# Key and query products of a graph-transformer layer from raw, feature-major rows, with the mean taken into the weights

## The chip, the cores and the metric

The kernel runs on one core of a Trainium2 chip. The metric is the device time of one execution in microseconds (us). A time is the median of several runs; a profile is one further execution, taken by the hardware profiler. The engines are TensorE (PE, with its weight loads as PEld), VectorE (DVE), ScalarE (ACT), GpSimd (POOL) and SyncE (SP), which only issues transfers. ACT and POOL issue transfers too.

## What is computed

One layer on N = 10000 nodes with D = 512 features, everything in 32-bit floats:

```python
xn  = layernorm(x)                       # no gamma; eps 1e-5
gnn = relu(segment_sum((xn @ W)[src] * edge_weight, dst) + bias)   # 160000 edges
q, k, v = split(xn @ w_qkv.T)            # 8 heads of 64
q = softmax(q over the 64 of its head) * 64**-0.5
k = softmax(k over the 10000 nodes)
mix = gamma_layernorm(((k.T @ v) per head applied to q) @ w_out.T)
x = x + gnn + mix
x = x + ffn(layernorm(x))                # two of eleven mixtures of six experts, gelu
```

## The kernel before

The nodes are cut into 20 chunks of 512 (the last has 272), each held as 128 partitions of 4 rows (`SUB`). The work runs in four stages.

**Early stage (chunks 0 and 1, `EARLY = 2`).** `normal_rows` loads a chunk of x, takes mean and variance of each row on DVE (`row_stats`), finishes the rate (variance + eps)^-0.5 and the shift on POOL, applies both on ACT (L422), and writes the normalised rows to `xn_d` in memory. It does so for all 20 chunks, seven buffers (`a_io`) turning over. Between these, DVE prepares the edge lists (`place_edges`), and the keys and queries of chunks 0 and 1 are made by plain products (`times`, L209).

**Key stage (chunks 2 to 19, line 856 on).** For each chunk the normalised rows are reloaded (`rows_of`), transposed on PE (`turned_rows`, which calls `transposed`, L201, and copies the result from PSUM to `xnT` on ACT and DVE, L203), and summed blockwise into `xs_b`. `seven` forms keys and queries with seven products instead of eight, from `xnT`, `xs_b`, the weights `wk` and `wq` and their blockwise sums `kq_sum`. ACT exponentiates, DVE adds keys up (`kacc`) and normalises queries. The next chunk's rows are then transposed, and the context `G` takes `ek` transposed times `xn` (`pc`, L911). Midway the queries are transposed and put away in `qT_d`.

The factor `usable` that scales the exponentials is 1 where the squared column norms of `wk` and `wq` are small enough for exponentials without a maximum, and 0 otherwise, when a general path recomputes everything.

**Attention stage.** The context is folded with the value and output weights; then for each chunk: queries times that (`po`), the collected messages times the graph weights (`pg`), norms and sums.

**Feed-forward stage**, from about 2143 us to the end; the change does not touch it.

**The edges.** Messages are gathered in 1250 tiles of 128 edges by POOL (`edges_in`, L583, one indirect transfer each, from `xn_d`, 24 buffers), multiplied on PE by a selection matrix (`edges_summed`, L601, four tiles side by side) and written out as partial sums. They are spread over the key and attention stages by a count kept while the program is written: `work(us)` adds the nominal time of the products just issued to `done[1]`, and `edges_to` issues edge tiles until their number matches `done[1] / pace`:

```python
edges_to(groups_of(int(done[1] / pace[0])))
```

with 0.83 us for a product of [128x128] by [128x512], `PACE = 0.9` us a tile in the key stage and `ROW_PACE` in the attention stage. At the start of the key stage `done[1]` is set to minus 16 tiles. In the attention stage `far_enough(c)` also forces out the tiles that the gather of chunk c's sums needs. PE's instructions run in the order in which the program writes them; the order on the other engines and queues is a planner's.

Of the kernel before, what the change touches and what calls it, by code (L numbers as in the profile page):

```python
# [9 lines left out]
F32 = mybir.dt.float32  # L10
I32 = mybir.dt.int32
AF = mybir.ActivationFunctionType
ALU = mybir.AluOpType
# [4 lines left out]
P = 128  # L18
SQ = 32
SPARE = 10  # L20
SUB = 4
# [7 lines left out]
EARLY = 2  # L29
# [3 lines left out]
KEPT = 2  # L33
PRODUCT = 0.83
PACE = 0.9
ROW_PACE = 0.96
LATE = 4
MIXED = 3

# [17 lines left out]
def gps_layer_kernel(  # L57
    ctx: ExitStack,
    tc: tile.TileContext,
    x: bass.AP,  # L60
    src: bass.AP,
    dst: bass.AP,
    edge_w: bass.AP,
# [13 lines left out]
    nc = tc.nc  # L77
# [21 lines left out]
    def tokens(t, c):  # L99
        b, r = chunks[c]  # L100
        return t[b : b + r * SUB, :].rearrange("(p s) d -> p s d", s=SUB)

    const = ctx.enter_context(tc.tile_pool(name="const", bufs=1))
    small = ctx.enter_context(tc.tile_pool(name="small", bufs=4))
    dram = ctx.enter_context(tc.tile_pool(name="dram", bufs=1, space=DRAM))
# [29 lines left out]
    row_of = const.tile([P, NCH], I32, name="row_of")  # L135
    msum = const.tile([P, 1], F32, name="msum")
    stats2 = const.tile([P, NCH, SUB, 2], F32, name="stats2")


    xn_d = dram.tile([N, D], F32, name="xn_d")  # L140
# [247 lines left out]
    with ExitStack() as ph:  # L388
# [15 lines left out]
        tmp = norm_ctx.enter_context(tc.tile_pool(name="edge_t", bufs=1))  # L404


        normal = []
        placing = []
        last_stats = [None]

        def normal_rows(n):

            for c in range(len(normal), min(len(normal) + n, NCH)):
                r = chunks[c][1]
                xt = (xp if c < KEPT else a_io).tile([P, SUB, D], F32, name="xn")
                nc.sync.dma_start(xt[:r], tokens(x, c))
                mv = small.tile([P, SUB, 2], F32, name="mv")
                last_stats[0] = row_stats(xt, r, mv, on_pool=True)
                nc.gpsimd.tensor_tensor(mv[:r, :, 0], mv[:r, :, 0], mv[:r, :, 1], ALU.mult)
                nc.gpsimd.tensor_scalar(mv[:r, :, 0], mv[:r, :, 0], -1.0, None, op0=ALU.mult)  # L420
                for i in range(SUB):
                    nc.scalar.activation(xt[:r, i, :], xt[:r, i, :], AF.Identity,  # L422
                                         bias=mv[:r, i, 0:1], scale=mv[:r, i, 1:2])
                nc.scalar.dma_start(tokens(xn_d, c), xt[:r])
                normal.append(xt)
                if len(normal) == LISTS:
                    placing.append(place_edges(*edges_listed()))
                for _ in range(2 if placing else 0):
                    next(placing[0], None)

        zero = tmp.tile([P, D], F32, name="zero")
        nc.vector.memset(zero, 0.0)
        nc.scalar.dma_start(part_d[ZERO_ROW : ZERO_ROW + P, :], zero)
        normal_rows(2)
        src_sb = ep.tile([P, NET], I32, name="src_sb")
        w_sb = ep.tile([P, NET], F32, name="w_sb")
# [172 lines left out]
        nexts = ep.tile([P, 1], F32, name="nexts")  # L609
        held = {"edges": []}  # L610

        def squares_of(w, tag):
            sq = b_io.tile([P, KB, D], F32, name="sq", tag=tag)
            nc.scalar.activation(sq, w, AF.Square)
            return sq

        def norms(i, sq):

            pn = psum_e.tile([P, KB], F32, name="pn", tag="pm")
# [78 lines left out]
        def work(us):  # L698
# [4 lines left out]
                normal_rows(int(done[1] / EARLY_TOTAL * (NCH + 1)) + 4 - len(normal))  # L703
                return
            edges_to(groups_of(int(done[1] / pace[0])))

        in_order = ph.enter_context(ExitStack())
        in_order.enter_context(tc.manual_schedule(engines={mybir.EngineType.PE}))

        def general_path():  # L710

# [122 lines left out]
            nc.sync.dma_start(xn[: chunks[c][1]], tokens(xn_d, c))  # L834
            return xn

        def turned_rows(c, xn):
            xnT = b_io.tile([P, KB, SUB * P], F32, name="xnT")
            transposed(xnT, xn, chunks[c][1], psum, "ps", by_act=range(KB) if c < EARLY else (1, 3))
            return xnT  # L840

        def finish(o, ek, r, at):
            if o is ek:
                nc.vector.tensor_tensor(kacc[:r], kacc[:r], ek[:r, at, :], ALU.add)
            else:
                softmax_rows(o, r, at)

        wk = kvp.tile([P, KB, D], F32, name="wk")
        nc.sync.dma_start(wk, w_qkv_t[:, D : 2 * D].rearrange("(k p) d -> p k d", p=P))
        nc.sync.dma_start(wq, w_qkv_t[:, :D].rearrange("(k p) d -> p k d", p=P))  # L850
        squared = [squares_of(wk, "qT"), squares_of(wq, "xs_b")]
        kq_sum = kvp.tile([P, 4, KH, D], F32, name="kq_sum", tag="wv_wo")
        normal_rows(2)
        xn = rows_of(0)
        xnT = turned_rows(0, xn)
        for c, (_, r) in enumerate(chunks):
            if c == EARLY:
                for _ in placing[0]:
                    pass
                norm_ctx.close()  # L860
                pools["w"] = edge_ctx.enter_context(tc.tile_pool(name="edge_w", bufs=3))
                done[1] = -16 * PACE
                pools["m"] = edge_ctx.enter_context(tc.tile_pool(name="edge_m", bufs=24,
                                                                 reuse_waits="tile"))
            if c + 1 < EARLY:
                xn_next = rows_of(c + 1)
            elif EARLY <= c < NCH - 1:
                xn_next = rows_of(c + 1)
            ek = b_io.tile([P, SUB, D], F32, name="ek")
            qt = b_io.tile([P, SUB, D], F32, name="qt")  # L870
            if c < EARLY:
                for o, w in ((ek, wk), (qt, wq)):
                    sums = []
                    for s in range(SUB):
                        po = psum.tile([P, D], F32, name="pk", tag="ps")
                        times(po, xnT, s, r, w)
                        work(KB * PRODUCT)
                        sums.append(po)
                        if c == s == 0 and o is ek:
                            norms(0, squared[0])  # L880
                            norms(1, squared[1])
                            as_they_are()
                        for i, po in enumerate(sums):
                            at = s + 1 - len(sums) + i
                            nc.scalar.activation(o[:r, at, :], po[:r], AF.Exp, scale=usable[:r])
                            finish(o, ek, r, at)
                        sums = []
            else:
                xs = b_io.tile([P, 4, KH, HALF], F32, name="xs_b")
                h = 2 * r  # L890
                sums_of([xs[:, i, :, :h] for i in range(4)], xnT[:, :KH, :h], xnT[:, KH:, :h],
                        xnT[:, :KH, h : 2 * h], xnT[:, KH:, h : 2 * h])
                for s in range(SUB // 2):
                    first = seven(ek, qt, s, r, xnT, xs, (wk, wq), kq_sum, lambda n: work(n * KH * PRODUCT))
                    s2 = s + SUB // 2
                    nc.scalar.activation(ek[:r, s, :], first, AF.Exp, scale=usable[:r])
                    nc.scalar.activation(ek[:r, s2, :], ek[:r, s2, :], AF.Exp, scale=usable[:r])
                    finish(ek, ek, r, s)
                    finish(ek, ek, r, s2)
                    for q in (s, s2):  # L900
                        nc.scalar.activation(qt[:r, q, :], qt[:r, q, :], AF.Exp, scale=usable[:r])
                        finish(qt, ek, r, q)
            if c + 1 == EARLY:
                normal_rows(NCH)
                xn_next = rows_of(c + 1)
            if c + 1 < NCH:
                xnT = turned_rows(c + 1, xn_next)
            for cb in range(KB):
                pc = psum.tile([P, D], F32, name="pc", tag="ps")
                for s in range(SUB):  # L910
                    nc.tensor.matmul(pc, ek[:r, s, cb * P : (cb + 1) * P], xn[:r, s, :],  # L911
                                     start=s == 0, stop=s == SUB - 1)
                if c:
                    added = nc.vector.tensor_tensor(G[:, cb, :], G[:, cb, :], pc, ALU.add)
                    if cb == 0:
                        first_added = added
                else:
                    nc.vector.tensor_copy(G[:, cb, :], pc)
                work(SUB * PRODUCT)
                if cb == KB // 2 - 1:  # L920
                    qT = b_io.tile([P, KB, SUB * P], F32, name="qT")
                    transposed(qT, qt, r, psum, "ps", by_act=range(KB) if c < EARLY else (1, 3))
                    nc.scalar.dma_start(qT_d[c], qT[:, :, : SUB * r])
            if c == CHECKED:
                next_nodes()
                oddities()
            if c >= CHECKED:
                find_rows(c, added)
                if c < 2 * CHECKED:
                    find_rows(c - CHECKED, added)  # L930
            if c == EARLY - 1:
                for inst in sums_for([kq_sum[:, i] for i in range(4)], wk[:, :KH], wq[:, :KH], wk[:, KH:], wq[:, KH:]):
                    behind(inst, first_added)
            if c + 1 < NCH:
                xn = xn_next
# [537 lines left out]
```

## Time and profile before

| | us |
|---|---|
| median of 3 runs | 3301.59 (3297.64 to 3308.94) |
| the profiled execution | 3518.48 |
| its span, first to last instruction | 3516.7 |
| PE / DVE / ACT / POOL busy in it | 3256.7 / 1766.5 / 831.1 / 1311.2 |
| mean granted PE clock | 0.961 of full |

The profiled execution is 217 us longer than the median of the runs; its durations serve for a sum over its own stages. A page's rows give, for each group of instructions, source line, engine, operation, tiles written and read, count, busy time and mean duration, then the idle time of the engine just before them and what ended it. Rows in order of time begin with start and duration in us. A busy PE is not PE at its peak, since matmuls are pipelined and their ends modelled, so distances from start to start are used here.

### The profile page before, as it was taken

What the parts mean: (1) busy time and instruction counts of PE and PEld (TensorE: products, weight loads), DVE (VectorE), ACT (ScalarE), POOL (GpSimd) and SP (SyncE); (2) the same over time, 40 slices, a digit from 0 to 9 for tenths busy, and PEclk for the clock granted to TensorE, in tenths of its full rate; (3) what the DMA queues carried; (4) which work ended last, traced back from release to release, by engine and by line L of the source; (5) the groups of instructions that cost most, each with busy time, mean ns of one, the idle gap of its engine ahead of it and who ended that gap; (6) DMA issues with size and microseconds to landing.
All of it is one profiled execution on the core that took longest, in us unless ns stands there. A gap on an engine that the chain in (4) does not pass through costs nothing. (4 is left out here: it accounts for less than half of the span.)

```text
span 3516.7 us, 36142 instructions
## 1 busy us (share of the span) xinstructions
PE 3256.7 (93%) x12819; PEld 1916.0 (54%) x12819; DVE 1766.5 (50%) x3902; ACT 831.1 (24%) x1674; POOL 1311.2 (37%) x1421
## 2 busy tenths in 40 slices
PE   6899998988999989898998988999999999999998
PEld 3433333333333333333333335888888888888886
DVE  6644445444444425564565557445445544544542
ACT  5321212121112112121222113222222222222221
POOL 3466666665666656676676630000000000000000
PEclk8999999999999979899999988999999999999999
DMA  9677777776777878898998882221212212122111
GB/s 392 235 217 249 227 247 248 254 223 208 227 223 243 247 275 318 313 332 293 318 336 301 294 268 61 60 75 58 60 57 76 60 49 84 49 60 73 60 37 38
DMA packets 216735, 654.39 MB, mean 186 GB/s; under 512 B 34425, under 2 KB 74361, under 8 KB 188831
## 3 DMA queue, kind: packets, MB, share of 16 engines
q0 software_dynamic: 104096, 354.29, 32.0%
q1 hardware_dynamic: 69992, 175.33, 15.2%
q10 hardware_dynamic: 42452, 122.31, 9.0%
q8 instruction: 105, 1.72, 0.2%
q14 instruction: 90, 0.74, 0.1%
HBM read 491.21 MB, written 166.63 MB: 187 GB/s over the span
## 5 line engine op out<-in xcount | busy, mean ns | idle before, releaser
L583 POOL DMA_INDIRECT msg<-xn_d,src_sb x1250 | 1229.9, 984 | 634.4 <-issue 287.2
L601 PE MATMUL pm<-msg,sel 128*32 128x512 f32 x2504 | 351.7, 617 | 54.5 <-issue 44.5
L911 PE MATMUL pc<-xn,ek 128*128 128x512 f32 (+1 forms) x640 | 306.5, 624 | 20.5 <-issue 15.0
L209 PE MATMUL po<-G,qT 128*128 128x512 f32 (+1 forms) x640 | 302.0, 613 | 13.0 <-issue 12.2
L209 PE MATMUL pg<-wq,aT 128*128 128x512 f32 (+1 forms) x640 | 301.3, 617 | 10.2 <-issue 9.0
L604 ACT COPY part<-pm 128x512 f32<-128x512 f32 x217 | 127.1, 586 | 733.9 <-PE pm L601 276.0
L601 PEld LDWEIGHTS pm<-msg,sel 128*32 128x32 f32 x2504 | 66.1, 110 | 302.7 <-issue 266.2
L209 PEld LDWEIGHTS pg<-wq,aT 128*128 128x128 f32 (+1 forms) x640 | 117.7, 192 | 195.7 <-issue 184.7
L911 PEld LDWEIGHTS pc<-xn,ek 128*128 128x128 f32 (+1 forms) x640 | 122.7, 199 | 177.4 <-issue 164.7
L209 PEld LDWEIGHTS po<-G,qT 128*128 128x128 f32 (+1 forms) x640 | 117.4, 191 | 185.6 <-issue 181.4
L243 PE MATMUL px<-xnT,w_sb 128*128 128x256 f32 (+1 forms) x800 | 204.6, 379 | 6.8 <-DVE u L1290 6.8
L243 PE MATMUL p<-kq_sum,xs_b 128*128 128x512 f32 (+1 forms) x432 | 201.4, 600 | 3.2 <-issue 2.4
L166 DVE BATCH_NORM_STATS2 st<-ot 128x6 f32<-128x512 f32 (+1 forms) x160 | 110.3, 689 | 178.5 <-issue 119.2
L243 PE MATMUL px<-w_sb,hh 128*128 128x256 f32 (+1 forms) x800 | 185.7, 379 | 0.0
L243 PE MATMUL py<-xs,w_sum 128*128 128x256 f32 (+1 forms) x800 | 185.3, 374 | 0.0
L243 PE MATMUL p<-wk,xnT 128*128 128x512 f32 (+1 forms) x288 | 148.1, 637 | 34.9 <-issue 26.7
L243 PE MATMUL py<-w_sum,hh 128*128 128x256 f32 (+1 forms) x800 | 179.2, 379 | 0.0
L589 DVE TENSOR_TENSOR sel<-iota_w,place 128x128 f32<-128x128 f32 (+2 forms) x217 | 74.5, 344 | 206.1 <-remote 86.2
L243 PEld LDWEIGHTS px<-xnT,w_sb 128*128 128x128 f32 x800 | 150.7, 192 | 29.9 <-DVE u L1290 10.0
L243 PEld LDWEIGHTS py<-w_sum,hh 128*128 128x128 f32 (+1 forms) x800 | 150.0, 188 | 22.7
L243 PEld LDWEIGHTS px<-w_sb,hh 128*128 128x128 f32 (+1 forms) x800 | 150.0, 188 | 22.7
L243 PEld LDWEIGHTS py<-xs,w_sum 128*128 128x128 f32 x800 | 149.8, 190 | 19.9
(298 smaller groups left out, 4577.4 us busy)
## 6 DMA issues: line engine op xcount, KB each, us to landing
part_d<-part ACTq DMA_DIRECT2D x217, 256.0 KB
msg<-xn_d,src_sb POOLq DMA_INDIRECT x1250
xn<-in_x SPq DMA_DIRECT2D x19, 1024.0 KB
xn_d<-xn ACTq DMA_DIRECT2D x19, 1024.0 KB
qT_d<-qT ACTq DMA_DIRECT2D x19, 1024.0 KB
qT<-qT_d SPq DMA_DIRECT2D x19, 1024.0 KB
xt<-in_x SPq DMA_DIRECT2D x19, 1024.0 KB
x_d<-ot SPq DMA_DIRECT2D x19, 1024.0 KB
```

The source lines that it names most:

```text
L166: nc.vector.bn_stats(st[:r, s, :], t[:r, s, :])
L209: nc.tensor.matmul(po[:r, :], t[:, kb, s * r : (s + 1) * r], w[:, kb, :], start=kb == 0, stop=kb == KB - 1)
L243: nc.tensor.matmul(o, lhs[j], rhs[j], start=start and j == 0, stop=stop and j == n - 1, skip_group_check=True)
L583: nc.gpsimd.indirect_dma_start(out=m[k], out_offset=None, in_=xn_d, in_offset=bass.IndirectOffsetOnAxis(ap=src_sb[:, t0 + k : t0 + k + 1], ...
L589: nc.vector.tensor_tensor(sel[:, :n], iota_w[:, None, :].to_broadcast([P, n, WIN]), place[:, t0 : t0 + n, None].to_broadcast([P, n, WIN]), ...
L601: nc.tensor.matmul(pm[h * WIN : (h + 1) * WIN, :], sel[:, k, :], m[k] if k < len(m) else m[0], start=j == 0, stop=j == batch - 1, skip_gro ...
L604: nc.scalar.copy(part, pm)
L911: nc.tensor.matmul(pc, ek[:r, s, cb * P : (cb + 1) * P], xn[:r, s, :], start=s == 0, stop=s == SUB - 1)
```

## The change

The host now also hands over `x_t`, the values of x laid out by feature: for each chunk and each block of 128 features one row per feature, the tokens in the chunk's own order. `turned_rows` no longer transposes; it loads 1 MB of `x_t` into `xnT`. These rows are raw. Since k = rate * (x - mean(x)) @ W, the mean is moved to the weights: `centred` subtracts from each column of `wk` and `wq` its mean over the 512 features (a product with `all_ones`, then four updates on DVE). The rate of each token, kept in `stats1`, becomes the scale of the exponentials, multiplied by `usable`. The weights and the first chunk of `x_t` are loaded ahead of the normalised rows. The normalised rows themselves are still made, for the edges and for `pc`. Two constants of the edge schedule change: minus 49 tiles at the start of the key stage instead of minus 16, and `ROW_PACE` 0.94 instead of 0.96.

```diff
-ROW_PACE = 0.96
+ROW_PACE = 0.94
...
+    def columns(t, c):
+        b, r = chunks[c]
+        return t[:, KB * b : KB * (b + r * SUB)].rearrange("p (k n) -> p k n", k=KB)
...
+    stats1 = const.tile([P, NCH, SUB, 2], F32, name="stats1")
+    nc.gpsimd.memset(stats1, 0.0)
...
-                mv = small.tile([P, SUB, 2], F32, name="mv")
+                mv = stats1[:, c]
                 last_stats[0] = row_stats(xt, r, mv, on_pool=True)
...
+        def turned_rows(c):
+            xnT = b_io.tile([P, KB, SUB * P], F32, name="xnT")
+            nc.sync.dma_start(xnT[:, :, : SUB * chunks[c][1]], columns(x_t, c))
+            return xnT
+
+        def centred(w):
+
+            pcol = psum.tile([P, D], F32, name="pcol", tag="ps")
+            for kb in range(KB):
+                nc.tensor.matmul(pcol, all_ones, w[:, kb, :], start=kb == 0, stop=kb == KB - 1)
+            for kb in range(KB):
+                nc.vector.scalar_tensor_tensor(w[:, kb, :], pcol, -1.0 / D, w[:, kb, :], op0=ALU.mult, op1=ALU.add)
+
         zero = tmp.tile([P, D], F32, name="zero")
         nc.vector.memset(zero, 0.0)
         nc.scalar.dma_start(part_d[ZERO_ROW : ZERO_ROW + P, :], zero)
+        wk = kvp.tile([P, KB, D], F32, name="wk")
+        nc.sync.dma_start(wk, w_qkv_t[:, D : 2 * D].rearrange("(k p) d -> p k d", p=P))
+        xnT = turned_rows(0)
+        nc.sync.dma_start(wq, w_qkv_t[:, :D].rearrange("(k p) d -> p k d", p=P))
+        squared = [squares_of(wk, "qT"), squares_of(wq, "xs_b")]
+        centred(wk)
         normal_rows(2)
...
-        def turned_rows(c, xn):
-            xnT = b_io.tile([P, KB, SUB * P], F32, name="xnT")
-            transposed(xnT, xn, chunks[c][1], psum, "ps", by_act=range(KB) if c < EARLY else (1, 3))
-            return xnT
...
-        wk = kvp.tile([P, KB, D], F32, name="wk")
-        nc.sync.dma_start(wk, w_qkv_t[:, D : 2 * D].rearrange("(k p) d -> p k d", p=P))
-        nc.sync.dma_start(wq, w_qkv_t[:, :D].rearrange("(k p) d -> p k d", p=P))
-        squared = [squares_of(wk, "qT"), squares_of(wq, "xs_b")]
         kq_sum = kvp.tile([P, 4, KH, D], F32, name="kq_sum", tag="wv_wo")
         normal_rows(2)
         xn = rows_of(0)
-        xnT = turned_rows(0, xn)
         for c, (_, r) in enumerate(chunks):
             if c == EARLY:
...
+                rates = ep.tile([P, NCH, SUB], F32, name="rates")
+                nc.vector.tensor_scalar(rates, stats1[:, :, :, 1], usable, None, op0=ALU.mult)
                 norm_ctx.close()
                 pools["w"] = edge_ctx.enter_context(tc.tile_pool(name="edge_w", bufs=3))
-                done[1] = -16 * PACE
+                done[1] = -49 * PACE
...
+                    if c == 0 and o is qt:
+                        centred(wq)
...
+                        if s == 0 and o is ek:
+                            rate = small.tile([P, SUB], F32, name="rate")
+                            nc.vector.tensor_scalar(rate[:r], stats1[:r, c, :, 1], usable[:r], None, op0=ALU.mult)
...
-                            nc.scalar.activation(o[:r, at, :], po[:r], AF.Exp, scale=usable[:r])
+                            nc.scalar.activation(o[:r, at, :], po[:r], AF.Exp, scale=rate[:r, at : at + 1])
...
-                    nc.scalar.activation(ek[:r, s, :], first, AF.Exp, scale=usable[:r])
-                    nc.scalar.activation(ek[:r, s2, :], ek[:r, s2, :], AF.Exp, scale=usable[:r])
+                    nc.scalar.activation(ek[:r, s, :], first, AF.Exp, scale=rates[:r, c, s : s + 1])
+                    nc.scalar.activation(ek[:r, s2, :], ek[:r, s2, :], AF.Exp, scale=rates[:r, c, s2 : s2 + 1])
...
-                        nc.scalar.activation(qt[:r, q, :], qt[:r, q, :], AF.Exp, scale=usable[:r])
+                        nc.scalar.activation(qt[:r, q, :], qt[:r, q, :], AF.Exp, scale=rates[:r, c, q : q + 1])
...
-                xnT = turned_rows(c + 1, xn_next)
+                xnT = turned_rows(c + 1)
```

More of the change, by code (lines that the diff above doesn't have):

```diff
@@ L60, in gps_layer_kernel @@
     x: bass.AP,
+    x_t: bass.AP,
     src: bass.AP,
@@ L404, in gps_layer_kernel @@
         tmp = norm_ctx.enter_context(tc.tile_pool(name="edge_t", bufs=1))
+        in_order = ph.enter_context(ExitStack())
+        in_order.enter_context(tc.manual_schedule(engines={mybir.EngineType.PE}))
         normal = []
@@ L429, in normal_rows, with squares_of @@
                     next(placing[0], None)
+        def squares_of(w, tag):
+            sq = b_io.tile([P, KB, D], F32, name="sq", tag=tag)
+            nc.scalar.activation(sq, w, AF.Square)
+            return sq
+        def turned_rows(c):
[8 more added lines that the diff above has]
+                nc.vector.scalar_tensor_tensor(w[:, kb, :], pcol, -1.0 / D, w[:, kb, :], op0=ALU.mult, op1=ALU.add)
         zero = tmp.tile([P, D], F32, name="zero")
@@ L610, in gps_layer_kernel @@
         held = {"edges": []}
[L612 to L615, printed above, removed]
         def norms(i, sq):
@@ L705, in work @@
             edges_to(groups_of(int(done[1] / pace[0])))
-        in_order = ph.enter_context(ExitStack())
-        in_order.enter_context(tc.manual_schedule(engines={mybir.EngineType.PE}))
         def general_path():
@@ L1446 @@
         "x": x,
+        "x_t": np.concatenate([x[b : b + SUB * P].reshape(-1, SUB, x.shape[1] // P, P).transpose(3, 2, 1, 0).reshape(P, -1)
+                               for b in range(0, x.shape[0], SUB * P)], axis=1),
         "src": by_tile(src),
```

## The prediction

> **What bounds the kernel now.** I read the page first, then windows, waits and order of time within each stage. The chain of waits followed back from the end covers only the last stage, which the change does not touch, so it says nothing here. The 40 slices show where the touched part lies:
>
> ```profile
> PE   6899998988999989898998988999999999999998
> POOL 3466666665666656676676630000000000000000
> DMA  9677777776777878898998882221212212122111
> ```
>
> TensorE is nearly full everywhere. GpSimd gathers messages from slice 2 to slice 24, at 60 to 70% of *busy* time, and its pause between gathers is not in that figure. The first slice is full of transfers. The windows of the early part sharpen this:
>
> ```profile
> 30.00:40.00 10.00, 8.28 (x32) 4.98 (x32) 6.81 (x21) 6.91 (x11) 4.89 (x11) 0.69 1.01 428
> 90.00:100.00 10.00, 0.00 (x0) 0.00 (x0) 10.00 (x37) 2.93 (x4) 3.54 (x6) 0.54 0.90 375
> ```
>
> The columns are PE, PEld, DVE, ACT, POOL, granted clock, DMA share and GB/s. Up to 100 us the early stage lives from the transfers (about 425 GB/s) and, at 90 us, from VectorE. Next, PE in order of time, where the early stage starts, ends, and in one key chunk (c >= 2):
>
> ```profile
> 31.72 5.91 PE L209 MATMUL pk<-wk,xnT 128*128 128x512 f32 x8 [13.29 <-ACT xnT L203]
> 100.73 0.90 PE L201 MATMUL pt<-ident,qt 128*128 128x128 f32 x3 [13.32 <-DVE G L918]
> 159.87 1.88 PE L243 MATMUL p<-kq_sum,xs_b 128*128 128x512 f32 x4
> ...
> 728.35 1.91 PE L201 MATMUL pt<-ident,xn 128*128 128x128 f32 x16
> 730.10 3.60 PE L911 MATMUL pc<-xn,ek 128*128 128x512 f32 x8
> 733.62 1.92 PE L601 MATMUL pm<-msg,sel 128*32 128x512 f32 x16
> ```
>
> From start to start, the 16 transposes that the change removes hold PE for 730.10 - 728.35 = 1.75 us. Eight records of pc (each product of two [128x128]x512 operands leaves two records) take 3.52 us, so 0.44 a record, 0.43 where nothing else intervenes, 0.86 a product. Eight edge tiles (16 records) take 1.86, so 0.232 a tile; in the attention stage they come in fours at 1.0, so 0.25. Last, the gathers:
>
> ```profile
> 724.09 0.95 POOL L583 DMA_INDIRECT msg<-xn_d,src_sb  x1 [0.30 <-issue]
> 725.34 0.95 POOL L583 DMA_INDIRECT msg<-xn_d,src_sb  x1 [0.30 <-issue]
> ```
>
> One gather every 1.25 us, whenever POOL is free to go. What POOL waits for, in the key stage (142 to 1225 us) and then in the attention stage (1310 to 2060); the numbers are us in total, times, longest:
>
> ```profile
> POOL msg L583 <- PE pm L601: 124.5, 68, 12.9
> ```
>
> ```profile
> POOL msg L583 <- PE pm L601: 17.6, 27, 2.0
> ```
>
> These are waits for a message buffer that PE has yet to read. So in the key stage POOL waits for PE, and **PE is the bound with POOL close behind**; in the attention stage POOL hardly ever waits for PE, and the two are about level.
>
> **The Trainium skill.** "TensorE: Matmul & The Clock Gate", Part 4: PE-mode transpose, gives about 275 ns for a 128x128 transpose inside a kernel. The groups of instructions agree on the single one, 281 ns:
>
> ```profile
> L201 PE MATMUL pt<-ident,xn 128*128 128x128 f32 (+1 forms) x320 | 41.9, 281 | 18.5 <-ACT xn L422 14.0 <-issue 3.8 <-DVE xnT L203 0.8
> ```
>
> But these overlap, and 16 advance PE by only 1.75 us, so I use 0.109 and not 0.28. The same page, Part 1: The HAM clock gate, says that PE runs at half clock after an idle window. The trace agrees: 8 records took 5.91 us at 31.72 us, after 13 us of idling, against 3.60 later. "DMA: Bandwidth & Descriptors", Bandwidth, has 1 MB into 128 partitions at 6.15 us (issued from GpSimd), and its section on queues, rings and completion order says that engines alternate between queues by packet. The trace has no landing time for a plain load amid gathers, so this page is my lower price for one.
>
> **The change, part by part**
>
> *A. The start.* PE now waits for the first normalised chunk, then for four copies queued on ACT, until 31.72. Afterwards wk and the raw chunk 0 head SP's queue. The first two x loads are read by DVE from 7.47 and 10.68 us, so 3.2 us a load: wk at about 7.5, x_t at 10.7, wq at 13.9. The column sum (8 records, 5.91 cold) and four VectorE updates of 0.75 (nearest row: 128x512 scalar_tensor_tensor, 749 ns) put the first pk at about 14 to 16 us, 16 to 18 earlier. Added on PE later: wq's column sum, 3.4. Taken away: 32 transposes, 3.5 or more. `usable` comes earlier too, so ACT's 15.77 us wait for it shrinks. But not all arrives at chunk 2: the exponentials of chunk 1 stand behind the last normalised rows on ACT, and the rows are bound by transfers. Two raw chunks ahead of them are 2 MB / 425 GB/s = 4.9 us more. Before, the last x load landed at 129.10 and chunk 2 began at 159.87, 31 later; that load was issued only at 114.33, behind a load that waited for pc of chunk 0. About 46 MB (20 read, 18 written, 4 of weights and raw chunks, 2.5 of edge lists, the rest small) at 0.42 MB a us take 110 us, the earliest for it now; plus 31 gives 141. So PE reaches chunk 2 at about 140: **-20** (between 0 and -40).
>
> *B. Key chunks.* 18 x 1.75 = **-31.5** of PE. The copies that followed (36 of 0.66 on DVE, 44 of 0.58 on ACT) lie beside PE and count nothing. The exponentials take a token's rate where `usable` stood, an operand of the same shape, and `rates` and the memset of stats1 are one small instruction each: nothing, beside PE. Each chunk adds a 1 MB load on SP, into a single buffer: it can start when the products of chunk c are read, and must be in place, with three sums of 0.69, when pc is done: from 730.10 to 749.68, 19.6 us. At the page's 6.15 alone, or 1 MB in the idle quarter of the transfers (this stage moves 233 GB/s at a share of 0.74, so 82 GB/s are idle: 12.8 us), plus 2.1 of sums, it is covered. I take nothing; the ends are -3 (no more waits of PE on ACT's xnT copies: 5.0 us seen once) and the first rival.
>
> *C. Edges moved.* A key chunk counts 44 x 0.83 = 36.5 us of work, 18 of them 657; /0.9 = 730 tiles. The start offset takes 16 of these before and 49 after, so in whole groups 712 against 680: 32 tiles leave, 32 x 0.232 = **-7.4**; in the attention stage they cost 32 x 0.25 = **+8**.
>
> *D. The late bursts.* Counting the loop out with ROW_PACE, tile 1184 is reached after attention chunk 14 before, 1132 after; the gather of each later chunk then forces the rest. So 118 tiles instead of 66 fall in some 2.5 chunks. PE has 2.5 x (32 x 0.86 + 1.75) = 73 us of other work there, plus 118 x 0.25 = 30: 103. POOL needs 118 x 1.25 = 148, less up to 24 tiles gathered ahead (30): 118. Some 15 short, and bursts are uneven: **+20** (0 to +45). Before, 66 x 1.25 = 83 fits in 89.
>
> Sum: -20 - 31.5 - 7.4 + 8 + 20 = **-31 us**. Against the profiled execution's own 3518.5 (span 3516.7) that is 3487.6. The median of the timed runs is 3301.6, 217 lower; the last stage (2142.57 to the end) is gapless on PE, so the difference must lie before it, in stalls that I did not count as gain. I carry the -31 over as it stands: 3270.6.
>
> **Rivals**
>
> 1. *The load comes late.* If SP puts x_t behind the next xn load, which needs the buffer that pc frees, PE waits after every pc for at least 6.15 + 2.1 us: 17 x 8.3 = 141, less A and B: +90, 3391. It decides from a landing of 17 us on. For it: one buffer, and SP did once put a blocked load first (113.89). Against: 19.6 us of cover.
>
> 2. *POOL becomes the bound.* After the change a key chunk holds 44 x 0.86 + 1.75 = 39.6 us of products and qT transposes for 40.6 tiles, so PE spends 0.975 + 0.232 = 1.21 us a tile, below POOL's 1.25. If POOL, fed by rows that are ready no earlier, sets the pace, A and B vanish, and the 32 postponed tiles are paid on POOL in the attention stage: 32 x 1.25 = +40, less 20 of slack: 3322. It decides where POOL's waits for PE are near nothing in the key stage. For it: 1.25 against 1.21. Against: 124.5 us of such waits now.
>
> 3. *A wash.* POOL bound as above, but rows ready some 20 us earlier: 3301.
>
> 4. *Larger gain.* Chunk 2 at 120 instead of 140, no bursts: 3235.
>
> **How the numbers follow.** A measurement of this kernel tells 0.3% (10 us) from no change. My forecast (3250 to 3292) 0.48, the larger gain 0.17, the wash 0.12, POOL as bound 0.17, the late load 0.06. Faster 0.65, same 0.12, slower 0.23. The predicted time is that of the likeliest, 3271. The range reaches from the larger gain to POOL as bound, 3232 to 3322; the late load and half of the outer edges are left out.
>
> **What would show it.** A: first pk near 15 us, the first product of kq_sum near 140. B: no xnT transpose, no wait of PE or DVE for the x_t load, and POOL's waits for PE in the key stage well below 124. D: PE waiting for messages around the last three edge chunks. A sum of xs_b that waits for the x_t load in every chunk, or a key stage as long as before with POOL never waiting, would prove me wrong.

## The result and the profile after

| | us | ratio to before |
|---|---|---|
| before, median of 4 runs | 3301.28 (3297.64 to 3308.94) | 1 |
| after, median of 4 runs | 3353.45 (3342.45 to 3358.93) | 1.0155 (95% interval 1.0136 to 1.0173) |
| after, the profiled execution (span 3340.7) | 3342.45 | |
| before, profiled a second time (span 3296.8) | 3298.5 | |

The change makes the kernel 52 us slower; the prediction was 31 us faster. After's profiled execution is the fastest of its four, 11 us below the median. The only profile of before that the prediction had was an execution 217 us longer than the runs, so before was profiled once more, and from here on "before" is this second profile, which took as long as the runs. The slices of after:

```profile
PE   6699999999999999999998889999999999999998
POOL 3427777777777777777676500000000000000000
DMA  9748989988888999999998841212121221212111
```

and of before, second profile:

```profile
PE   6899999999999999999998979999999999999998
POOL 3377777777776677777776300000000000000000
```

In after, POOL drops to 2 in the third slice (167 to 251 us) and goes on longer in the slice where its gathers end. Early after, PE in order of time (start, duration, then engine, line, operation, tiles, count, and in brackets the idle time before it and what ended it):

```profile
15.56 3.70 PE L216 MATMUL pk<-wk,xnT 128*128 128x512 f32 x8 [0.85 <-DVE wk L457]
...
89.22 0.45 PE L208 MATMUL pt<-ident,qt 128*128 128x128 f32 x1 [18.84 <-DVE qt L201]
...
159.21 0.45 PE L208 MATMUL pt<-ident,qt 128*128 128x128 f32 x1 [6.58 <-DVE qt L201]
...
172.58 1.88 PE L250 MATMUL p<-kq_sum,xs_b 128*128 128x512 f32 x4
...
227.64 1.92 PE L635 MATMUL pm<-msg,sel 128*32 128x512 f32 x16
```

The first key product comes at 15.56, as predicted. But chunk 2, predicted for 140, starts at 172.58 (159.77 in before), and the first edge product only at 227.64. What POOL does meanwhile, in order of time:

```profile
139.37 1.26 POOL L617 DMA_INDIRECT msg<-xn_d,src_sb  x1 [15.61 <-issue]
...
228.96 0.94 POOL L617 DMA_INDIRECT msg<-xn_d,src_sb  x1 [56.97 <-PE pm L635]
```

POOL fills its 24 message buffers from 139.37 to 172 and then stands for 56.97 us, until PE reads the first message. POOL's waits for a free buffer in the key stage of after (142 to 1150 us; total, times, longest), and in that of before (142 to 1225 us):

```profile
POOL msg L617 <- PE pm L635: 81.9, 72, 57.0
```

```profile
POOL msg L583 <- PE pm L601: 32.4, 76, 4.4
```

Without that one wait after has 24.9. In before the 124.5 us of the first profile have shrunk to 32.4, of which most are ordinary pauses of 0.3: **POOL has hardly any slack in an execution as long as the runs.** The gathers and the edge products of after, from the groups of instructions (busy us, mean ns, idle before):

```profile
L617 POOL DMA_INDIRECT msg<-xn_d,src_sb x1250 | 1236.0, 989 | 477.5 <-issue 222.9
L635 PE MATMUL pm<-msg,sel 128*32 128x512 f32 x2504 | 403.1, 610 | 41.3 <-DMA msg<-xn_d,src_sb 40.0
```

and of before:

```profile
L583 POOL DMA_INDIRECT msg<-xn_d,src_sb x1250 | 1235.3, 988 | 430.0 <-issue 209.7
L601 PE MATMUL pm<-msg,sel 128*32 128x512 f32 x2504 | 361.7, 605 | 19.1 <-DMA msg<-xn_d,src_sb 17.5
```

The gathers cost POOL the same; the same 1250 edge products keep PE "busy" for 41 us more and leave it 22 us more idle. That is waiting, some of it counted as busy. It is plain at the weight loads (PEld). The weights of an edge product are the selection matrix `sel` (128x32) and the message (128x512) is its other operand, but the weight load is the record at which the wait for the message stands. These waits, over the whole of before and of after:

```profile
PEld pm L601 <- DMA msg<-xn_d,src_sb: 66.7, 83, 4.0
```

```profile
PEld pm L635 <- DMA msg<-xn_d,src_sb: 124.7, 135, 6.9
```

58 us more of waiting for messages, against 14 us less of everything else (3342.45 - 124.7 = 3217.8, and 3298.5 - 66.7 = 3231.8). In the prediction's profile this wait was 5.4 us.

### The profile page after: what moved, and what is told of

Same layout as the page of the kernel before. It is cut to its first block, busy times and chain, and to the rows that moved or that the text cites. A ratio compares the mean times of both kernels' runs of the same rounds, so it can differ in the third digit from the quotient of the medians.

```text
span 3340.7 us, 35485 instructions
## 1 busy us (share of the span) xinstructions
PE 3201.8 (96%) x12515; PEld 1876.5 (56%) x12515; DVE 1757.2 (53%) x3877; ACT 809.2 (24%) x1630; POOL 1316.5 (39%) x1422
## 3 DMA queue, kind: packets, MB, share of 16 engines
q1 hardware_dynamic: 73256, 195.81, 17.5%
## 5 line engine op out<-in xcount | busy, mean ns | idle before, releaser
L635 PE MATMUL pm<-msg,sel 128*32 128x512 f32 x2504 | 403.1, 610 | 41.3 <-DMA msg<-xn_d,src_sb 40.0
L216 PE MATMUL po<-G,qT 128*128 128x512 f32 (+1 forms) x640 | 290.3, 599 | 0.0
L216 PE MATMUL pg<-wq,aT 128*128 128x512 f32 (+1 forms) x640 | 289.0, 601 | 0.0
L934 PE MATMUL pc<-xn,ek 128*128 128x512 f32 (+1 forms) x640 | 286.5, 597 | 0.0
L635 PEld LDWEIGHTS pm<-msg,sel 128*32 128x32 f32 x2504 | 75.4, 109 | 337.1 <-issue 187.0
L250 PEld LDWEIGHTS px<-xnT,w_sb 128*128 128x128 f32 x800 | 149.8, 191 | 27.0 <-DVE u L1313 7.4
L250 PEld LDWEIGHTS p<-kq_sum,xs_b 128*128 128x128 f32 (+1 forms) x432 | 78.6, 188 | 117.1 <-issue 94.5
```

Of the source, the lines that this page charges most:

```text
L216: nc.tensor.matmul(po[:r, :], t[:, kb, s * r : (s + 1) * r], w[:, kb, :], start=kb == 0, stop=kb == KB - 1)
L250: nc.tensor.matmul(o, lhs[j], rhs[j], start=start and j == 0, stop=stop and j == n - 1, skip_group_check=True)
L635: nc.tensor.matmul(pm[h * WIN : (h + 1) * WIN, :], sel[:, k, :], m[k] if k < len(m) else m[0], start=j == 0, stop=j == batch - 1, skip_gro ...
```

## The experiments

All times in one table; the diffs follow. "POOL idle" sums the gaps of more than 0.5 us ahead of a gather, between the first and the last one. "PEld wait" is the wait for messages just shown. "Rest" is the profiled execution less this wait. The ratios are to before, on the same chip. Where a text below counts PE from start to start, it sums the distances between the starts of its products, from the first of chunk 2 to the last of the attention stage.

| run | median us | ratio (95% interval) | POOL idle | PEld wait | rest |
|---|---|---|---|---|---|
| before (e0) | 3298.5, one run | | 43.6 | 66.7 | 3231.8 |
| after | 3353.45 | 1.0155 (1.0136 to 1.0173) | 86.9 | 124.7 | 3217.8 |
| e1_off16 | 3308.97 | 1.0031 (1.0019 to 1.0042) | 62.5 | 95.3 | 3216.2 |
| e2_before49 | 3344.85 | 1.0136 (1.0119 to 1.0153) | 76.7 | 103.1 | 3242.5 |
| e3_off0 | 3297.82 | 1.0001 (0.9992 to 1.0010) | 54.5 | 85.6 | 3214.0 |
| e4_before_half | 3232.71 | 0.9799 (0.9781 to 0.9817) | 758 | none shown | 3233.5 |
| e5_off0_half | 3215.12 | 0.9748 (0.9729 to 0.9766) | 719 | none shown | 3215.6 |
| e6_off0_trans | 3300.46 | 1.0002 (0.9993 to 1.0011) | 50.3 | 51.1 | 3251.5 |
| e7_off0_order | 3296.51 | 0.9993 (0.9985 to 1.0002) | 42.5 | 79.2 | 3216.6 |
| e8_ahead16 | 3287.19 | 0.9954 (0.9937 to 0.9971) | 38.9 | 77.6 | 3211.2 |
| e9_off0_order4 | 3290.34 | 0.9966 (0.9953 to 0.9980) | 38.1 | 88.8 | 3203.0 |
| e10_ahead16_order4 | 3280.78 | 0.9939 (0.9926 to 0.9952) | 30.5 | 80.1 | 3200.7 |

**e0_before: before, profiled again.** No edit.

> The kernel before, unchanged, for a second profile: the first profiled execution was 217 us longer than the runs, so the stages of the changed kernel need one of about 3300 us to stand beside. Theory (GpSimd's gathers are the bound in both kernels): in a profile near 3300 us the gathers follow one another at about 1.35 us a tile with hardly a wait for PE, and last from about 155 us to about 1845. Rival (PE is the bound before, the changed kernel loses by PE's own waits): POOL's waits for a buffer that PE has to read still come to 100 us or more in the key stage.

3298.5 us, within 1 us of the median of 3298.91 on its chip. The 18 runs of before on this chip lie between 3293.62 and 3303.98, so the 217 us belong to that one execution; what made it longer stays open. In the new profile the gathers run from 149.7 to 1845.2 us: 1695.6, of which 1235.3 are gathers, 373.1 the pauses of at most 0.5 between them, 43.5 POOL's other transfers with the gaps ahead of them, and 43.6 idle. POOL is occupied for 97% of its stretch, though its busy share of that stretch is only some seven tenths.

**e1_off16 and e2_before49: the start offset.**

```diff
# e1_off16, from after
-                done[1] = -49 * PACE
+                done[1] = -16 * PACE
# e2_before49, from before
-ROW_PACE = 0.96
+ROW_PACE = 0.94
-                done[1] = -16 * PACE
+                done[1] = -49 * PACE
```

> The changed kernel with the edge schedule's start put back from minus 49 tiles to minus 16 (ROW_PACE stays 0.94). Theory: in the changed kernel POOL fills its 24 buffers by 172 us and then stands idle until 229, since the first edge products come only at 228; 33 tiles earlier is some 37 us earlier, all of it gained: about 3316. Rival (PE bound; the loss is PE's late arrival at chunk 2 and the waits for x_t): PE's work is the same in another order, 3345 to 3355.

> The kernel before with only the two constants of the change: minus 49 tiles and ROW_PACE 0.94. Theory: the first edge products come some 36 us later while the first gathers do not, so POOL idles for 25 to 36 us more: 3326 to 3337. Rival: PE has no less and no more to do, within 10 us of 3301, or up to 20 slower by the late bursts that the prediction counted.

With 16 in place of 49, after is 10 us slower than before instead of 52; with the two constants alone, before becomes 46 us slower. Both effects go the way of the theory and are somewhat larger than it said (37, and 25 to 36). POOL's stand at its 25th gather, in e1 and in e2, in order of time:

```profile
195.76 0.94 POOL L617 DMA_INDIRECT msg<-xn_d,src_sb  x1 [23.41 <-PE pm L635]
```

```profile
218.27 0.94 POOL L583 DMA_INDIRECT msg<-xn_d,src_sb  x1 [34.69 <-PE pm L601]
```

The stand is 57 in after, 23 in e1, 35 in e2, 2 in before. So the constants account for nearly all of the loss, most of it by letting POOL stand idle at the start. In e2 "rest" grew by 11 as well; there TensorE's weight loads wait 12.7 us for ACT to clear the partial sums, 3.0 in before. (e1 keeps `ROW_PACE` at 0.94; that constant alone was not tried.)

**e3_off0: no offset at all.**

```diff
-                done[1] = -49 * PACE
+                done[1] = 0.0
```

> The changed kernel with the edge schedule starting at 0 tiles. Theory: edge products begin right at chunk 2, about 175 us, when the 24 buffers have just filled; POOL hardly idles, 50 to 57 us gained: about 3300, no more than the kernel before, since POOL's own time then sets the end. Rival: as for minus 16, 3345 to 3355, or slower, as PE waits for the first messages.

3297.82: all of the loss is gone, but nothing is gained, although 288 transposes have left PE. PE and then POOL in order of time:

```profile
171.35 1.88 PE L250 MATMUL p<-kq_sum,xs_b 128*128 128x512 f32 x4
...
183.47 1.92 PE L635 MATMUL pm<-msg,sel 128*32 128x512 f32 x16
```

```profile
184.78 0.94 POOL L617 DMA_INDIRECT msg<-xn_d,src_sb  x1 [12.68 <-PE pm L635]
```

The late chunk 2 still costs POOL 12.68 us. The next three runs ask where the 31.5 us of transposes went.

**e4_before_half and e5_off0_half: half the gathers.** Every second gather is left out, and the edge product reads the message before it again; PE's instructions stay.

```diff
-                    if k < n:
+                    if k < n and k % 2:
+                        m[k] = m[k - 1]
+                    elif k < n:
```

> The kernel before with every second message gather left out (the odd tile of a pair takes the even tile's messages, so the sums over edges are not those of the reference); PE's work is unchanged. Theory (gathers are the bound): POOL needs about half, PE becomes the bound with its 0.86 us a product, and the time falls by 60 to 100 us, to 3200 to 3240. Rival (PE bound already): falls by less than 15 us.

> The changed kernel with the edge schedule from 0 tiles and every second message gather left out in the same way. Set beside the kernel before with the same left out, it shows what the change is worth where PE is the bound. Theory: 18 x 1.75 = 31.5 us of transposes less, PE's arrival at chunk 2 some 12 us later (172 against 160 in the profiles): 15 to 25 us faster than the kernel before so treated. Rival (the change has a cost of its own in the key stage, the load of x_t): no faster, or slower.

Before falls by 67.5 us to 3232.71, and after with no offset by 82.7 to 3215.12: the version with the change is now 17.6 us the faster. No wait for messages is left, and the edge products' row shows what they cost PE without one, here in e5:

```profile
L637 PE MATMUL pm<-msg,sel 128*32 128x512 f32 x2504 | 313.8, 601 | 0.0
```

So of the 403.1 in after 89.3 came of waiting; with the 40.0 shown as idle, 129.3, close to PEld's 124.7. And "rest" in the full versions (3231.8 in before, 3214.0 in e3) is what e4 and e5 measure outright (3233.5 and 3215.6 in their profiled executions): in these two pairs the time is PE's own path plus the wait for messages, to 2 us.

One rival is left. Half the gathers are also less work for the transfer engines. Before and then e4, from 1200 to 1800 us (the last two columns are the DMA share and GB/s):

```profile
1200.00:1800.00 600.00, 593.01 (x2066) 222.78 (x2065) 369.08 (x957) 133.32 (x256) 449.33 (x450) 0.99 0.96 342
```

```profile
1200.00:1800.00 600.00, 597.19 (x2194) 229.56 (x2187) 385.30 (x997) 142.93 (x276) 226.79 (x232) 1.00 0.76 254
```

A gather takes POOL as long in both (0.99 us in before, 629.9 / 625 = 1.01 in e4), so POOL's own pace does not come from full transfer engines. But no run lightens the transfers alone, so it is not shown that they have no part in PE's waits for messages.

**e6_off0_trans: the transposes put back, for nothing.** After with no offset; the 16 transposes a chunk are issued again and their results not used.

```diff
+            if EARLY <= c + 1 < NCH:
+                rn = chunks[c + 1][1]
+                for kb in range(KB):
+                    pt = psum.tile([P, SUB * P], F32, name="pt", tag="ps")
+                    for s in range(SUB):
+                        nc.tensor.transpose(pt[:, s * rn : (s + 1) * rn],
+                                            xn_next[:rn, s, kb * P : (kb + 1) * P], ident[:rn, :rn])
```

> The changed kernel with the edge schedule from 0 tiles, and PE's 16 transposes of each next chunk's rows put back in the key stage, their results unused (no copies): 18 x 1.75 = 31.5 us more on PE. Theory: POOL sets the pace, PE has that much idle time: within 5 us of 3298. Rival (PE bound): 3325 to 3330.

3300.46 against 3297.82, ratios of 1.0002 and 1.0001: from start to start all transposes take PE 99.6 us against 71.3 in e3, 28.3 more, and the kernel does not show it. The edge products take 352.0 against 383.0, 31.0 less. PEld's wait for messages goes down in the same way, from 85.6 to 51.1:

```profile
PEld pm L635 <- DMA msg<-xn_d,src_sb: 51.1, 67, 3.8
```

**This is where the expected gain went.** Read the other way, what PE saves in the key stage comes back as waiting for the next message.

**e7_off0_order: the sum behind the softmax, a miss.** In after, DVE stands for 23.34 us at the first sum of chunk 2, and chunk 1's queries, queued behind it, are what PE waits for at 159.21. DVE in order of time:

```profile
154.50 0.69 DVE L233 TENSOR_TENSOR xs_b<-xnT 128x512 f32<-128x512 f32 x1 [23.34 <-DMA xnT<-in_x_t]
...
156.96 1.27 DVE L199 TENSOR_REDUCE qs<-qt 128x8 f32<-128x512 f32 x2
```

e7 orders the first of the four sums (`sums_of`) behind the last query softmax of the chunk before (`behind` gives the planner an order between two instructions).

```diff
# with no offset; sums_of returns its first sum, softmax_rows its last instruction
-                softmax_rows(o, r, at)
+                held["query"] = softmax_rows(o, r, at)
-                sums_of([xs[:, i, :, :h] for i in range(4)], ...)
+                behind(sums_of([xs[:, i, :, :h] for i in range(4)], ...), held["query"])
```

> The changed kernel with the edge schedule from 0 tiles, and VectorE's sums of a chunk's x_t ordered behind the softmax of the chunk before (in the changed kernel VectorE stood for 23 us at the first such sum, waiting for the load, with chunk 1's queries queued behind it). Theory: chunk 2 starts 5 to 10 us earlier, edge products with it, and POOL's idle time of 12.7 us at full buffers shrinks by as much: 3288 to 3293. Rival (this wait is covered): 3298.

3296.51, not told from e3. The edit missed: the planner put the second sum where the first had been.

```profile
154.20 0.69 DVE L234 TENSOR_TENSOR xs_b<-xnT 128x512 f32<-128x512 f32 x1 [22.19 <-DMA xnT<-in_x_t]
```

**e8_ahead16, e9_off0_order4, e10_ahead16_order4: both remedies.** In e8 the edges start 16 tiles ahead; in e9, with no offset, all four sums are ordered; e10 has both.

```diff
# e8_ahead16 and e10_ahead16_order4
-                done[1] = -49 * PACE
+                done[1] = 16 * PACE
# e9_off0_order4 and e10_ahead16_order4; sums_of returns its four sums
-                sums_of([xs[:, i, :, :h] for i in range(4)], ...)
+                for inst in sums_of([xs[:, i, :, :h] for i in range(4)], ...):
+                    behind(inst, held["query"])
```

> The changed kernel with the edge schedule starting 16 tiles ahead (plus 16 instead of minus 49). With a start at 0 POOL still stood 12.7 us with full buffers, until the first edge product at 183 us. Theory: the first edge product comes some 8 us earlier, at 175, and the time falls by as much below the 3298 of a start at 0: 3288 to 3292, faster than the kernel before. Rival (PE, given edges before its first key products, waits for messages): 3298 or more.

> As the last, a start at 0, but all four sums of a chunk's x_t ordered behind the softmax of the chunk before; with only the first of them ordered, VectorE stood for 22 us at the second. Theory: PE begins chunk 2 at 162 to 166 instead of 171, POOL's wait with full buffers falls from 12.7 to about 5: 3289 to 3293. Rival (the sums, now later, hold up PE at each of the 18 chunks, or POOL's other waits grow): 3296 or more.

> Both together, a start at plus 16 tiles and the four sums ordered. Theory: POOL has no wait for full buffers in the start any more, 12 us less than with a start at 0: 3285 to 3290. Rival: no better than either alone.

e10 has the lowest median, 0.6% below before (0.5 to 0.7%); e8 and e10 are not told apart by their intervals. PE in e10, in order of time:

```profile
153.12 1.91 PE L208 MATMUL pt<-ident,qt 128*128 128x128 f32 x16
...
161.73 1.90 PE L250 MATMUL p<-kq_sum,xs_b 128*128 128x512 f32 x4
...
165.28 3.64 PE L635 MATMUL pm<-msg,sel 128*32 128x512 f32 x32
```

The 16 query transposes run in one piece, chunk 2 begins 10 us sooner than in e3, and the first edges are read at 165, before the buffers are full. The order keeps its gain: in e9 PE ends the attention stage at 1905.3, in e3 at 1915.1.

**The earlier edges gain little by the way that was expected.** In e8 POOL's stand at the 25th gather falls from 12.68 to 4.09 us, and its last gather ends at 1823.8, 18.3 earlier than in e3. But the edges are also asked for earlier: from start to start they hold PE for 382.5 us, against 383.0, and after the last gather 89.5 us of the attention stage are left, against 73.0. PE ends that stage at 1913.3, only 1.8 us ahead of e3; in e10 it is 3.0 ahead of e9. The rest is gained behind it, where PE waits for the first rows of the feed-forward stage (which begins at 1925.56 us in before; the 2143 given above are of the first profile). In e3 and in e8:

```profile
PE px L250 <- DVE xs L242: 13.8, 1, 13.8
```

```profile
PE px L250 <- DVE xs L242: 3.0, 1, 3.0
```

This wait is 13.7 or 13.8 us in every run but e8 and e10 (2.7); the table's "rest" has it in it. In e8 the planner put ACT's normalising of these rows ahead of its last step for chunk 19's statistics, at 1902.62; in e3 it stands behind that step, at 1918.19. So e8 met its number, 3288 to 3292, mostly by luck, and about 11 of the 20 us that e10 lies below before come from this order. Before was not tried with earlier edges, so how much of e10's lead is due to the change itself is not shown. PEld still waits 80 us for messages in e10: the gathers still hold PE up.

## Why the prediction was wrong

**What bounds the kernel: wrong, and all else follows.** The prediction read "POOL waits for PE, 124.5 us" and concluded that PE is the bound. That held in the execution that it looked at and not in the one that took as long as the runs: in the second profile these waits are 32.4 and the wait for messages runs the other way, 66.7. Its own numbers could have shown this. After the last gather before needs 1455.8 us in the first profile and 1451.6 in the second; a run of 3301.6 must therefore end its gathers near 3301.6 - 2 - 1456 = 1844. From 149.8, where they begin, that is 1694 us, and POOL is occupied for 1229.9 (gathers) + 350 (pauses) + 60 (other transfers) = 1640 of them even in the first profile. The 54 us left is all the idle time that POOL can have had in a run, against 271 in that execution. The step that failed is "I carry the -31 over as it stands": stalls that the runs do not have were the very slack on which the bound rested. With POOL nearly full in the runs, PE's savings are worth nothing, and what delays the gathers is paid.

The Trainium skill, "Perfetto Trace Analysis", Identifying the Most-Contended Engine, says that matmul busy time does not tell how close TensorE is to its limit, and goes by the weight loads instead. The trace agrees on the busy time: 48 us of the 361.7 in before's edge row come of waiting (361.7 - 313.5, the row of e4). The same section takes the engine of highest occupancy for the most contended one. By weight loads that is still PE, at 58% of the span against POOL's 40%, yet more work on PE cost nothing (e6) and half of the gathers took 67.5 us off. Here the measurement decides: POOL's occupancy must include the pause of 0.30 us that follows each gather.

**A, the start (-20): wrong in sign, about +13.** PE does start at 15.56, near the estimate, and the first gather comes 10 us earlier (139.4 against 149.7). But chunk 2 is not tied to the rows by a fixed 31 us. PE stood 36.5 us for chunk 0's queries, while DVE worked off row statistics and edge lists; with 8.5 for chunk 1's this row shows 44.9:

```profile
PE pt L208 <- DVE qt L201: 44.9, 8, 18.8
```

For chunk 1's, DVE stood 23.3 us for `x_t` of chunk 2, with the queries behind it. SP issued that load at 145.80, once chunk 1 had freed the single buffer, and the sum began at 154.50. The prediction asked who waits for the load in a key chunk; at the seam between the stages it did not ask what is queued behind the waiting sum on DVE. e9 takes that part out, and chunk 2 begins 10 us earlier.

**B, the transposes (-31.5): right in size, worth nothing.** From start to start 28.3 us of transposes leave PE (e3 against e6), and the time changes by nothing that can be told. With half the gathers the two kernels differ by 17.6: 29.6 of transposes from start to start, less the later chunk 2 (171.65 against 160.65, 11) and 1 us in smaller terms. (The 275 ns that the prediction quotes for a transpose are given there for bf16; these are f32.)

**The single load buffer: right for PE, wrong for DVE.** The prediction named a sum of `xs_b` that waits in every chunk as a sign of being wrong, and it came: `xs_b` waits for `x_t` 18 times, 74.2 us in all, 23.3 of them at chunk 2. Inside the later key chunks PE never waits for the load, so there it costs nothing. From issue to use it takes 8.7 us at chunk 2, which lies between the two prices (6.15 from the Trainium skill, "DMA: Bandwidth & Descriptors", Bandwidth, and 12.8). Rival 1 is out.

**C, the edges moved (-7.4 + 8): the term that was missing.** It priced 33 postponed tiles on PE. On POOL they are time in which nothing is gathered: with 24 buffers and chunk 2 late, 57 us at one place. e1 leaves 10 of the 52 us, and e2 puts the two constants at 46.

**D, the late bursts (+20): there, mostly as a symptom.** PE's shown waits for messages are 40.0 us, 17.5 in before. Its working compared different chunks: in the traces the products of attention chunk 14 end behind 1180 edge tiles in before and behind 1160 in after, and 1128 is the count after chunk 13. That the edges are late at the end because POOL is late from the start fits e1 and e3, where the same `ROW_PACE` goes with 21.4 and 14.6 us.

**Rival 2 had the mechanism, not the size.** "POOL becomes the bound" was given 3322 and 0.17. It charged POOL's postponed tiles as 40 less 20 of slack; there were about 57 us of standing and little slack. And it said *becomes*, where the gathers had bound the kernel before.

The whole, in terms of POOL, from before (second profile) to after: first gather 10.3 earlier, idle 43.3 more, other transfers and their gaps 9.4 more, the gathers and pauses 2.6 more: +45.0, and the last gather ends at 1890.1 against 1845.2. After that 1450.6 and 1451.6 follow. The two profiled executions differ by 44; the medians by 52, and for the last 8 no profile was taken.

## What to carry to other kernels

Hold the profiled execution against the runs before its waits are read: where it is longer, its idle time is not the kernel's, and an engine that looks slack may be full once the surplus is taken out. Add up an engine's work with the pauses between its instructions over the stretch in which it works, and ask for each delay of its consumer how long its buffers last. A saving on an engine that waits for another was worth nothing here (e6), and a schedule that let the binding engine start late cost 46 us (e2). And where an edit meets its expected number, look up where in the trace the time was gained: e8 met its own at another place.

## What the runs showed of the hardware

A gather of 128 rows takes POOL 0.99 us with a pause of 0.30, and in the profiles of the ten kernels with all 1250 of them (before: the second profile) gathers and short pauses add up to 1607 to 1616 us, with the transposes on PE or without them, and with PEld waiting from 51.1 to 124.7 us.

A matmul record lasts 0.59 us here, while the two records of an edge tile take 0.23 us from start to start, so a short wait before an edge product lies under the record before it and counts as PE's busy time: 313.5 us for the edge products in e4, with no wait, and 403.1 in after. The waits of the weight loads show it nearly whole (124.7, where 403.1 - 313.8 + 40.0 = 129.3).
